# Two graph attention layers: the last two batches spread their head sums through TensorE

## Chip, core and metric

The kernel runs on one core of one Trainium2 chip. The metric is the device time of one execution in microseconds (us). It is given as the median of several runs; a profiled execution of the same program supplies the trace.

## What is computed

The input x holds 64 batches of 256 nodes with 512 features, and adj is one 256 x 256 adjacency matrix for all batches. Two layers follow each other, each with a layer norm in front and a residual around it. All is 32-bit floating point.

```python
h = relu(layernorm(x))                       # layer 0: graph attention
Wh = h @ W
logits = leaky_relu(Wh @ a_src [rows] + Wh @ a_dst [columns], 0.2)
x = x + softmax(where(adj, logits, -inf)) @ Wh

h = relu(layernorm(x))                       # layer 1: 8 heads of 64
q, k, v = h @ Wq.T + bq, h @ Wk.T + bk, h @ Wv.T + bv
attn = softmax(where(adj, q @ k.T / 8, -inf))   # per head
x = x + concat(attn @ v) @ Wo.T + bo
```

The change lies in the second half of layer 1: the division by the softmax sums, and the product with Wo.

## The kernel before

One batch is one group, so G is 64 and the groups are numbered 0 to 63. A group lives in a few stages, each written as a Python generator that issues some instructions and yields: loading, norms, edge weights and aggregation of layer 0 (`normalize0`, `weights0`, `aggregate0`, `transform0`), norm and transpose of layer 1 (`normalize1`, `transpose1`), projections (`project_qk`, `project_v`), `attention`, `scale` and `output`.

**The order is written by hand.** Lists such as `first_half` and `second_half` (L818 to L825) name stages with an offset: `(output, -2)` advances the output of the batch two behind the current one by one step. The loop at L845 walks through the lists for each iteration. Each engine then executes its own instructions strictly in the order in which they were issued, and waits where one needs data that is not there yet. An instruction that waits therefore holds up everything behind it on its engine.

**The seven products.** A product of 256 x 512 with a 512 x 512 weight is split into quarters and done with seven quarter products instead of eight. `combine` (L162) makes four sums of quarters of the left side (L167 to L170), on GpSimd except in batch 0. `products` (L173) issues the seven, each into one of eight PSUM banks. Two matmuls of L209 make one product of rows. VectorE adds each product to one or several quarters of the destination; for the output this is `add_to_rows` (L564).

**Attention.** For a pair of heads e, `scores` (L683) multiplies q and k into two PSUM banks (psc) and ScalarE takes the exponential into ex. `masks` (L701) multiplies ex by the mask twice (L703) and adds its two halves into sm (L705), on VectorE. `values(j)` (L708) multiplies two pairs of heads with v into pav, and ScalarE copies it to aT (L723). This is done for j = 0 and 1, so for four values of e, which hold eight heads. Before the second `values`, GpSimd adds the output bias to x (L734).

**Head sums.** After the second `values`, eight matmuls on 32 columns each (L742) sum sm over the nodes into psm: head pair e lands in rows 32e to 32e+31, sixteen equal rows for each of its two heads. VectorE takes the reciprocals rc (L750). SP then issues eight DMAs (L755), each of which reads one row of rc and writes it to the 64 partitions of a head in rb. In `scale`, VectorE multiplies aT by rb (L767), two operations of 128 x 512, and `combine` makes the quarter sums called as. `output` runs the seven products with Wo (po) and stores the two row blocks by DMA after the sixth and seventh (L780).

**The end.** In iterations 62 and 63 the same lists run, with the stages of missing batches left out. Iteration 64 runs `last` (L825):

```python
last = [A_OLD, A_OLD, A_OLD, O, O, O, O, O, O, O, AS]
```

A_OLD is the attention of the batch before, O the output of two before, AS the scaling of the batch before. So batch 63 finishes its attention, batch 62 then gets its seven outputs, and batch 63 is scaled; iteration 65 runs the ordinary lists once more, of which only the outputs of batch 63 are left.

## Time and profile before

| What | Value |
|---|---|
| median of 3 runs | 2987.39 us |
| lowest and highest | 2985.2, 2988.77 us |
| profiled run: time, span of the trace | 2984.37, 2982.6 us |
| mean granted TensorE clock | 0.993 |
| broadcasts rb<-rc (L755) | 512 of 64 KB, median 4.7 us from issue to landing |
| reciprocals (L750) | 64 of 1758 ns |
| masks (L703) | 512, mean 913 ns |
| scalings aT by rb (L767) | 128 of 128 x 512, mean 685 ns |
| additions of products (L564) | 889, mean 685 ns |

The span runs from the first to the last instruction. Engines are PE (matmuls of TensorE), PEld (its weight loads), DVE (VectorE), ACT (ScalarE), POOL (GpSimd) and SP (SyncE, here the queue that issues DMAs). Times within the trace count from the start of the span. In the trace every 32-bit matmul is recorded as two rows, so one product of L209 is four rows. The names are the program's; buffer numbers are left out, so that aT stands for both halves and all batches.

A line of a group shows what was written, what was read, the shape, the number, the busy time and the mean of one. Idle time before an instruction is put down to what came last. The chain of work that ended last is followed back from the final instruction, each step to what released it.

### The profile page before, as it was taken

To read this page: it belongs to the slowest core of one execution; us is meant where nothing else is said; L and a number is where in the kernel's file an instruction comes from. 1 tells how busy PE (TensorE), PEld (TensorE's weight loads), DVE (VectorE), ACT (ScalarE), POOL (GpSimd) and SP (SyncE) were. 2 spreads that over 40 slices of the span, in tenths; PEclk is the share of its full clock that TensorE was granted. 3 is DMA by queue.
4 is the path that set the end of the run, shared out by engine and by line. 5 is a ranking of instruction groups with operands and counts; after the bars stand their busy time and mean duration, and the time that the engine had idled before them with its cause. 6 is when DMAs were issued, how large, how long until landed. Compare 5 with 4: busy or idle time off the path is not lost.

```text
span 2982.6 us, 51508 instructions
## 1 busy us (share of the span) xinstructions
PE 2918.6 (98%) x19824; PEld 2496.8 (84%) x19824; DVE 2355.9 (79%) x3671; ACT 1252.3 (42%) x2972; POOL 1262.2 (42%) x1484
## 2 busy tenths in 40 slices
PE   5999999999999999999999999999999999999997
PEld 3878888888888888888888888888888888888885
DVE  3687888888888878878878878878878878878875
ACT  3444344344344443443443444444443443443431
POOL 2234544544544534534534534434435435435432
PEclk8999999999999999999999999999999999999999
DMA  4012122122122122122122122221221221221222
GB/s 141 12 33 43 29 36 43 29 36 43 26 40 37 28 43 36 30 44 35 31 43 33 32 43 32 34 43 31 35 43 30 36 43 29 36 43 30 29 29 37
DMA packets 83835, 112.46 MB, mean 38 GB/s; under 512 B 11906, under 2 KB 49794, under 8 KB 83586
## 3 DMA queue, kind: packets, MB, share of 16 engines
q1 hardware_dynamic: 82786, 107.00, 22.2%
q8 instruction: 160, 2.62, 0.3%
q0 software_dynamic: 800, 2.11, 0.2%
q14 instruction: 89, 0.73, 0.1%
HBM read 41.95 MB, written 33.55 MB: 25 GB/s over the span
## 4 chain that ended last, share of the span: by engine, by line
PE 96%; DVE 1%; DMA 1%; ACT 1%; POOL 0%; SPq 0%; issue 0%; DVEq 0%; POOLq 0%; ACTq 0%
PE pqk L218 27%; PE po L209 26%; PE pv L209 12%; PE psc L690 8%; PE pav L715 8%; PE pu L532 7%; PE psm L742 2%; PE pt L620 2%; PE ps L502 1%; PE prs L515 0%; PE pe L480 0%; SPq L755 0%; DMA rb<-rc 0%; DMA a_row<-in_L_gnn_a_dst_dram 0%; DVE x L564 0%
## 5 line engine op out<-in xcount | busy, mean ns | idle before, releaser
L564 DVE TENSOR_TENSOR x<-po,x 128x1024 f32<-128x1024 f32 x889 | 592.8, 685 | 113.5 <-PE po L209 93.4
L437 POOL TENSOR_SCALAR ve<-ssq 128x2 f32<-128x2 f32 x128 | 25.1, 196 | 1083.3 <-ACT h L426 803.5
L703 DVE TENSOR_TENSOR ex<-ex,maskT 128x512 f32<-128x512 f32 x512 | 447.0, 913 | 6.6 <-ACT ex L698 6.6
L698 ACT ACTIVATE ex<-psc 128x512 f32<-128x512 f32 x512 | 264.4, 603 | 124.0 <-PE psc L690 124.0
L723 ACT COPY aT<-pav 128x512 f32<-128x512 f32 x128 | 74.9, 585 | 524.2 <-PE pav L715 496.6
L218 PEld LDWEIGHTS pqk<-hs,wq_sb 128*128 128x128 f32 x2048 | 264.5, 192 | 9.8
L209 PE MATMUL po<-wo_sb,as 128*128 128x256 f32 x1024 | 269.1, 386 | 3.5 <-POOL as L168 3.5
L218 PE MATMUL pqk<-hs,wq_sb 128*128 128x128 f32 x2048 | 270.8, 276 | 0.0
L218 PE MATMUL pqk<-hs,wk_sb 128*128 128x128 f32 x2048 | 270.6, 275 | 0.0
L209 PE MATMUL pv<-wv_sb,hs 128*128 128x256 f32 x1024 | 263.8, 381 | 3.9 <-DVE x L564 3.9
L690 PE MATMUL psc<-qk 64*128 64x256 f32 x2048 | 255.8, 389 | 0.0
L466 DVE SCALAR_TENSOR_TENSOR junk<-h,wa 128x512 f32<-128x512 f32 x256 | 246.4, 963 | 11.6 <-ACT h L459 0.6
L715 PE MATMUL pav<-ex,v 128*64 128x256 f32 x2048 | 250.8, 386 | 4.3 <-DVE ex L703 4.3
L532 PE MATMUL pu<-em,h 128*128 128x256 f32 x1024 | 245.0, 383 | 8.4 <-POOL em L494 8.4
L649 ACT ACTIVATE p<-pqk,bias 128x128 f32<-128x128 f32 x256 | 73.0, 368 | 425.2 <-PE pqk L218 425.2
L218 PEld LDWEIGHTS pqk<-hs,wk_sb 128*128 128x128 f32 x2048 | 249.2, 192 | 0.0
L209 PE MATMUL po<-w_sb,us 128*128 128x256 f32 x1008 | 248.8, 380 | 0.0
L690 PEld LDWEIGHTS psc<-qk 64*128 64x128 f32 x2048 | 187.5, 187 | 67.6 <-ACT aT L723 25.9
L705 DVE TENSOR_TENSOR sm<-ex 128x512 f32<-128x512 f32 x256 | 228.3, 892 | 8.9
L750 DVE RECIPROCAL rc<-psm 128x256 f32<-128x256 f32 x64 | 112.5, 1758 | 155.1 <-PE psm L742 155.1
L532 PEld LDWEIGHTS pu<-em,h 128*128 128x128 f32 x1024 | 197.0, 193 | 36.1 <-POOL em L494 8.7
L167 POOL TENSOR_TENSOR hs<-hT 128x256 f32<-128x256 f32 x63 | 73.8, 1172 | 349.5 <-ACT hT L621 349.5
(193 smaller groups left out, 5953.5 us busy)
## 6 DMA issues: line engine op xcount, KB each, us to landing
x<-in_x_dram SPq DMA_DIRECT2D x64, 512.0 KB, 5.4
rb<-rc SPq DMA_DIRECT2D x512, 64.0 KB, 4.7
out_dram<-x SPq DMA_DIRECT2D x128, 256.0 KB, 2.0
wq_sb<-in_L_gnn_Wq_dram SPq DMA_DIRECT2D x4, 256.0 KB, 12.1
wk_sb<-in_L_gnn_Wk_dram SPq DMA_DIRECT2D x4, 256.0 KB, 10.1
w_sb<-in_L_gnn_W_dram SPq DMA_DIRECT2D x4, 256.0 KB, 6.6
wv_sb<-in_L_gnn_Wv_dram SPq DMA_DIRECT2D x4, 256.0 KB, 6.6
wo_sb<-in_L_gnn_Wo_dram SPq DMA_DIRECT2D x4, 256.0 KB, 6.0
```

Source lines behind the costliest of these rows:

```text
L209: nc.tensor.matmul(dst[:, 0:HD], left[:, c, :], wt[:, slot, c, :], start=c == 0, stop=c == 1)
L218: nc.tensor.matmul(dst[:, at : at + P], wt[:, slot, c, e * P : (e + 1) * P], left[:, c, :], start=c == 0, stop=c == 1,)
L466: nc.vector.scalar_tensor_tensor(junk, h[:, t, :], 1.0, wa[a], op0=ALU.mult, op1=ALU.mult, accum_out=dst[:, t : t + 1],)
L532: nc.tensor.matmul(pu[:, d, :], h[:, m, (dp + d) * P : (dp + d + 1) * P], em[:, m, :], start=(m == 0), stop=(m == NC - 1),)
L564: nc.vector.tensor_add(dst, src, dst)
L690: nc.tensor.matmul(psc[r][:, m, :], qk[rows, 2 + e % 2, m * P : (m + 1) * P], qk[rows, e % 2, :], start=True, stop=True,)
L698: nc.scalar.activation(ex[:, r, :, :], psc[r], AF.Exp, scale=SCALE)
L703: nc.vector.tensor_mul(ex[:, r, :, :], ex[:, r, :, :], maskT)
L705: nc.vector.tensor_add(sm, ex[:, :, 0, :], ex[:, :, 1, :])
L715: nc.tensor.matmul(pav[r * DH : (r + 1) * DH, i, :], v[j][:, m, at : at + DH], pair[i][:, r, m, :], start=(m == 0), stop=(m == NC - 1),)
L723: nc.scalar.copy(aT[j], pav)
L750: nc.vector.reciprocal(rc, psm)
```

## The change

It touches the last two batches, 62 and 63, and the order of the last iterations.

- A matrix pick (128 x 128) is made once, in the second iteration, by VectorE: in each block of 32 rows, its row 0 has ones in columns 0 to 63, and its row 16 has ones in columns 64 to 127.
- For batches 62 and 63 the eight DMAs are replaced by four matmuls, each with 32 rows of pick and 32 rows of rc, that write the reciprocals of a head pair to all 128 partitions of a PSUM bank (prb). Four of the eight banks hold them.
- `scale` then multiplies aT in four operations of 128 x 256 that read PSUM. The quarter sums of these two batches are made on VectorE.
- Head sums and reciprocals become a function, `head_sums`. For batch 63 it is called ahead of the second `values`, not after it.
- The step order: iteration 63 has a list of its own, in which the outputs of batch 62 (OL) stand between the value products, scores and masks of batch 63. The end is one iteration shorter. Its list, `end`, finishes batch 63.

```diff
-        def combine(a, name, g):
+        def combine(a, name, g, alone=False):
...
-            engine = nc.gpsimd if g else nc.vector
+            engine = nc.vector if alone or g == 0 else nc.gpsimd
...
+        pick = weights.tile([P, P], F32, tag="pick", name="pick")
+        def picks():
+            first = weights.tile([P, Q], F32, tag="first", name="first")
+            nc.vector.tensor_reduce(first, ident.rearrange("p (a q) -> p q a", q=Q), AX.X, ALU.add)
+            for r in range(2):
+                at = r * (Q // 2)
+                nc.vector.tensor_copy(
+                    pick[:, r * DH : (r + 1) * DH], first[:, at : at + 1].to_broadcast([P, DH])
+                )
...
             nc.vector.tensor_scalar(flag, pk, P - 0.5, None, op0=ALU.is_lt)
+            yield
+            picks()
+            yield
...
+                if j and g == G - 1:
+                    rc = head_sums(g, sums)
                 values(j, pair)
                 if j == 0:
                     yield
+            if g < G - 1:
+                rc = head_sums(g, sums)
+            if g < G - 2:
+                rb = work.tile([P, DC, N], F32, tag="rb", name=f"rb_{g}")
...
+            else:
+                yield
+                rb = [bank([P, N], f"prb_{g}_{e}") for e in range(DC)]
+                for e in range(DC):
+                    rows = slice(e * Q, (e + 1) * Q)
+                    nc.tensor.matmul(rb[e], pick[rows, :], rc[rows, :], start=True, stop=True)
+                outs[g] = aT, rb
+            yield
...
-            for j in range(2):
-                nc.vector.tensor_mul(aT[j], aT[j], rb[:, 2 * j : 2 * j + 2, :])
+            if g < G - 2:
+                for j in range(2):
+                    nc.vector.tensor_mul(aT[j], aT[j], rb[:, 2 * j : 2 * j + 2, :])
+            else:
+                for e in range(DC):
+                    part = aT[e // 2][:, e % 2, :]
+                    nc.vector.tensor_mul(part, part, rb[e])
...
-            outs[g] = a, combine(a, "as", g)
+            outs[g] = a, combine(a, "as", g, g >= G - 2)
...
-        last = [A_OLD, A_OLD, A_OLD, O, O, O, O, O, O, O, AS]
+        OL = (output, -1)
+        last = first_half + [
+            A_OLD, A, V, V, A, A_OLD, AS, V, V, V, OL, A, V, OL, V, OL, OL, A, A, OL, A, OL, OL, A,
+        ]
+        end = [A_OLD, A_OLD, AS, OL, OL, OL, OL, OL, OL, OL]
...
-        for i in range(G + 2):
+        for i in range(G + 1):
...
-            elif i == G:
-                todo = last
+            elif i >= G - 1:
+                todo = end if i == G else last
```

In the list `last`, A is the attention of batch 63: scores of the first four heads, two masks, values, scores of the other four, two masks. V is its value projection, and A_OLD and AS finish and scale batch 62.

## The prediction

> **What bounds the kernel now.** Three views, from coarse to fine. First the busy time of the page, then the clock row of its slices:

> ```profile
> PE 2918.6 (98%) x19824; PEld 2496.8 (84%) x19824; DVE 2355.9 (79%) x3671; ACT 1252.3 (42%) x2972; POOL 1262.2 (42%) x1484
> ...
> PEclk8999999999999999999999999999999999999999
> ```

> TensorE is busy from end to end. In the table by stretches, 100 to 2900 us has 2792 of 2800 us of matmuls at clock 1.00. Nothing that merely rearranges waits can pay there. The same table shows 15.6 of 20 us for 2940 to 2960 and 9.9 of 23 for 2960 to 2983, and the change works in exactly this tail. Second, the chain that ended last, cut to the tail (start, duration, what):

> ```profile
> 2934.88 0.47 SPq L755
> ...
> 2940.85 4.75 DMA rb<-rc
> ...
> 2945.82 0.69 DVE aT L767
> 2946.51 1.74 DVE ex L703 x2
> 2948.28 1.10 DVE sm L705
> 2949.38 2.27 DVE ex L703 x2
> ...
> 2954.47 1.77 DVE rc L750
> ...
> 2962.21 4.88 DMA rb<-rc
> ...
> 2967.32 0.70 DVE aT L767
> ...
> 2968.15 0.73 POOL as L167
> 2968.95 0.73 POOL as L168
> 2969.73 7.22 PE po L209 x24
> 2976.97 0.42 DVE x L564
> ```

> The reader is to see two round trips through the DMA queue, one for batch 62 and one for batch 63. VectorE makes the reciprocals, SP issues eight broadcasts (6.0 us from 2956.24 to 2962.21), the last needs 4.88 us to land, and only then does VectorE scale. GpSimd's sums follow. Third, what this does to TensorE's clock (stretch, its us, busy us of each engine, granted clock, DMA):

> ```profile
> 2944.00:2948.00 4.00, 1.64 (x12) 0.74 (x8) 2.18 (x3) 2.06 (x4) 1.27 (x2) 1.00 0.17 12
> ...
> 2964.00:2966.00 2.00, 1.80 (x4) 1.18 (x4) 0.05 (x1) 0.00 (x0) 0.00 (x0) 0.50 0.86 65
> ...
> 2970.00:2972.00 2.00, 2.00 (x5) 1.58 (x6) 0.16 (x1) 0.00 (x0) 1.04 (x2) 0.50 0.00 0
> ```

> The 3.5 us gap before 2964.20 left the clock at half, so most of the last seven products ran slowly. The 2.2 us gap at 2945 did not.

> [...] half after 3.5 us, full again at 2973.3. [...] the masks and sums of heads 4 to 7 take 6.90 us (2946.43 to 2953.33) beside GpSimd, where the same work for heads 0 to 3 took 3.9. [...] No row here shows row tiles of 32; psm, four column tiles of 32, does 16 rows in 1.0 us, which fits four at once.

> **The change part by part**, against the profiled span of 2982.6. Prices are distances between starts in the trace: a VectorE operation on 256 columns 0.34, on 512 0.60, on 1024 1.14, two masks and the wait of their sum 1.32 (2936.69 to 2938.01), a dependent 256-column step 0.46 (63.32 to 63.78); a product of L209 0.865; a VectorE reader starts 0.20 after such a product's slot, and TensorE 0.05 to 0.15 after VectorE's end.

> *Up to 2934.88 nothing moves.* The three operations that make pick run once in the second iteration. The trace has no reduction of that size; I bound the three between nothing and 1.2 us (a 128x512 sum averages 0.89, a 128x128 fill is 0.17, twice) and take nothing: TensorE leads there and VectorE idles 20%.

> *First stretch, VectorE's queue.* In front of the masks of batch 63 now stands s2v (L194), which waits for the second value product: 2934.88 + 2 x 0.865 + 0.20 = 2936.81. Before, the masks began at 2934.77; behind s2v wait both masks, sm and the four scalings. From 2936.81: s2v 0.34, masks 1.32, sm 0.60, four scalings out of PSUM (priced by L194, PSUM and SBUF in, 256 columns) 3 x 0.34 + 0.46, the four quarter sums 0.46 + 0.35 + 0.34 + 0.33, four value additions 0.34 + 0.46 + 0.34 + 0.34, the first output addition 1.14, masks 1.32, sm 0.60, the value addition L203 0.42: together 10.18, end 2946.99. TensorE meanwhile does pick's four matmuls (0.55 if four at once, 1.73 if one by one), three value products, then from the second scaling's end (2939.98) six products of 0.865 to 2945.17. With slow pick matmuls it would be 2946.1. Either way TensorE waits for L203, so their price is hidden here. The first value matmuls of heads 0 to 3 that need L203 start at 2947.14.

> *Second stretch.* Twelve of the sixteen pav rows 1.41, scores 1.93, the fifth output product 0.87 and 0.20 to its reader: 2951.55. On VectorE that addition stands ahead of the masks, which wait behind it although the exponentials of their first head pair are ready by 2950.8 (scores + 1.17, two of 0.52). Then 0.60 + 1.32 + 0.60 + 0.34 + 0.34 + 1.32 + 0.69 = 5.21, so the last sm ends at 2956.76 against 2953.33 before: **+3.43**. This is the price of moving seven outputs (6.05 us of TensorE, 4.24 of VectorE) out of the shadow of the second round trip, already net of the 3.0 us of GpSimd interference that goes with the quarter sums. GpSimd's bias addition for batch 63 moves up behind that of batch 62 (2.5 us from 2917.8), where TensorE hides it. Batch 62's two stores now meet an empty SP queue.

> *Third stretch, reciprocals to second output product.* From sm to reciprocals and their 1.77 us nothing changes: end 2959.67 instead of 2956.24. Before, 13.49 us passed from there to 2969.73. Now: pick's first matmul and its read 0.58, three more scalings 1.02, then 0.46 and 0.46 to the second quarter sum, its 0.42 and 0.11 to TensorE: 3.05; with pick's matmuls one by one 3.4. The value product moved behind the sums (1.88 from 2957.8, copy by ScalarE done at 2960.47) stays just inside. **-10.4** or **-10.1**.

> *Fourth stretch.* From the second output product to the last addition took 7.66 at half clock; six products at full clock are 5.19 + 0.20 + 0.42 = 5.81: **-1.85**. The 5.21 us from there to the end of the span stay.

> Sum: 3.43 - 10.44 - 1.85 = -8.9, or -8.5; I take **-8.7**, span 2973.9. The three timed runs lie between 2985.2 and 2988.8, the profiled one at 2984.4; from their median 2987.4 the forecast is **2978.7**. Within 0.2%, 6.0 us, a measurement of this kernel can hardly tell from no change.

> **The rivals.** *Half clock in the new gap.* From 2953.1 to 2956.9 TensorE has only three of eight psm matmuls, some 0.4 us. If that halves the clock, psm costs 0.56 more and pav runs until about 2962.0, when the clock returns; the scalings of its half wait, and the second output product starts at 2964.65 instead of 2962.7: gain 6.8, time 2980.6. If the outputs stay at half too, 2982.4. For it: 3.5 us sufficed before. Against: 2944 to 2952 had two such gaps and kept 1.00.

> *The interleaving costs more.* VectorE's queue is strict and I let it wait for TensorE only twice. If the whole moved output block stays uncovered, that is another 3 us or so (6.05 - 3.43 = 2.6, and small waits): 2981.7.

> *Slower.* The clock halves at the first wait (2945.2 to 2947.1) and the later gaps never let it recover. The chain then repeats its matmul time: 1.41 + 1.93 + 0.87 + 1.06 + 0.55 + 5.19 = 11.0, against a gain of 8.7: 2989.7. It decides once half clock covers 8.7 us of that chain. Against it: 2.2 us of gap kept full clock before.

> That the change might not act at all is excluded: the loop that issues the broadcasts now stands under g < G - 2.

> **How the numbers follow.** Forecast 0.55, half clock 0.22, costlier interleaving 0.18, slower 0.05. Faster by over 0.2% (under 2981.4): 0.55 + 0.14 + 0.05 = 0.74; within: 0.08 + 0.13 + 0.03 = 0.24; slower by more: 0.02. The range runs from 2976.0 (the forecast, the cheap bound, and the 1.8 us by which runs differ) to 2983.5 (both middle rivals, their halves at higher times).

> **What would show it.** Right: no transfer of rb after batch 61; s2v ahead of the masks at about 2936.8; the last sm some 3.4 us later than before; about 3 us from the reciprocals' end to the second output product; the last seven products at clock 1.00 and 0.87 apart. Wrong: VectorE waiting for output products more than twice before the last sm, pick's matmuls above 1.7 us, or a clock of 0.5 after 2953.

## The result and the profile after

The changed kernel took 2974.19 us (median of four runs, 2974.02 to 2977.06) against 2986.84 us beside it, a ratio of 0.996 [0.9942, 0.9977]. The forecast was 2978.7 us, the range 2976.0 to 2983.5: right in direction, but the time lies 1.8 us below the range. The same changed kernel was compared with the one before three more times (the last two beside the same runs of the kernel before), with medians of 2978.52, 2978.54 and 2979.21 us and ratios of 0.9975 [0.9966, 0.9983], 0.9971 [0.9961, 0.9982] and 0.9974 [0.9964, 0.9984]. So the forecast meets the time of the later comparisons, and the question is what made the first one 4 us shorter.

The page after, busy times:

```profile
PE 2917.0 (98%) x19840; PEld 2492.8 (84%) x19840; DVE 2355.8 (79%) x3686; ACT 1252.5 (42%) x2972; POOL 1254.1 (42%) x1476
```

TensorE has sixteen more rows (two times eight for pick), GpSimd lost the eight quarter sums, and nothing else is to be seen at this scale. The chain that ended last, cut to the tail (start, duration, what):

```profile
2938.16 0.42 DVE s2v L194
...
2948.40 1.52 PE pav L730 x12
...
2952.94 0.69 DVE x L579
...
2957.46 0.70 DVE sm L720
...
2958.20 1.05 PE psm L785 x10
2959.25 1.88 PE pav L730 x16
...
2961.20 0.72 PE prb L776 x8
...
2964.38 5.43 PE po L209 x24
...
2969.84 0.42 DVE x L579
```

Both DMA round trips are gone. Between the reciprocals and the second output product stands pick's matmul of 0.72 us where a transfer of 4.88 us stood. The stretch table (stretch, its us, busy us and rows of PE, PEld, DVE, ACT and POOL, granted clock, DMA share, GB/s) shows the last products at full clock; from 169 to 2974.5 us this trace has no half clock:

```profile
2964.00:2966.00 2.00, 1.62 (x8) 1.47 (x9) 2.00 (x4) 0.00 (x0) 0.00 (x0) 1.00 0.00 0
2966.00:2968.00 2.00, 2.00 (x11) 1.77 (x10) 1.90 (x4) 0.00 (x0) 0.00 (x0) 1.00 0.03 8
```

To compare executions I cut each at the first scores of batch 63 (psc, right behind the head sums of batch 62). What lies ahead is the **start and the body**, what lies behind is the **tail**. Before, the scores begin at 2932.95 and the tail is 49.65 us. After, they begin at 2934.13, although the only work added far ahead of them is pick, and the tail is 40.87. (Spans are read to 0.1 us, so a tail is good to about 0.05.) The tail became 8.8 us shorter, for 8.7 forecast. What the forecast did not see is that the place of the scores is not a constant.

### The profile page after: what moved, and what is told of

Its sections match the earlier page's. It is cut to its first block, busy times and chain, and to the rows that moved or that the text cites. A ratio compares the mean times of both kernels' runs of the same rounds, so it can differ in the third digit from the quotient of the medians.

```text
span 2975.0 us, 51505 instructions
## 1 busy us (share of the span) xinstructions
PE 2917.0 (98%) x19840; PEld 2492.8 (84%) x19840; DVE 2355.8 (79%) x3686; ACT 1252.5 (42%) x2972; POOL 1254.1 (42%) x1476
## 4 chain that ended last, share of the span: by engine, by line
PE 96%; DVE 2%; ACT 1%; DMA 1%; POOL 0%; issue 0%; DVEq 0%; POOLq 0%; ACTq 0%
PE pqk L218 27%; PE po L209 26%; PE pv L209 12%; PE psc L705 8%; PE pav L730 8%; PE pu L547 7%; PE psm L785 2%; PE pt L635 2%; PE ps L517 1%; PE prs L530 0%; PE pe L495 0%; DVE x L579 0%; DMA a_row<-in_L_gnn_a_dst_dram 0%; DVE ex L718 0%; PE pgram L352 0%
## 5 line engine op out<-in xcount | busy, mean ns | idle before, releaser
L209 PE MATMUL po<-wo_sb,as 128*128 128x256 f32 x1024 | 268.3, 385 | 0.9 <-DVE as L168 0.9
L209 PE MATMUL pv<-wv_sb,hs 128*128 128x256 f32 x1024 | 263.4, 380 | 3.1 <-DVE x L579 3.1
L705 PE MATMUL psc<-qk 64*128 64x256 f32 x2048 | 256.0, 389 | 0.0
L209 PE MATMUL po<-w_sb,us 128*128 128x256 f32 x1008 | 248.6, 379 | 0.0
L705 PEld LDWEIGHTS psc<-qk 64*128 64x128 f32 x2048 | 187.5, 187 | 68.2 <-ACT aT L738 25.9
L167 POOL TENSOR_TENSOR hs<-hT 128x256 f32<-128x256 f32 x63 | 73.7, 1170 | 349.3 <-ACT hT L636 349.3
```

Of the source, the lines that this page charges most:

```text
L209: nc.tensor.matmul(dst[:, 0:HD], left[:, c, :], wt[:, slot, c, :], start=c == 0, stop=c == 1)
L705: nc.tensor.matmul(psc[r][:, m, :], qk[rows, 2 + e % 2, m * P : (m + 1) * P], qk[rows, e % 2, :], start=True, stop=True,)
```

## The experiments

Two theories of the missing 4 us were open after the result. A: the start of the program takes a different time in each execution. B: the tail of the kernel before is often longer than in its profile. A rival, C: something that the change adds shortens the start. The parts of the tail were tested beside them.

**Both kernels unchanged, and pick alone.** The third kernel is the one before with pick made and not used:

```diff
+        pick = weights.tile([P, P], F32, tag="pick", name="pick")
+        def picks():
...
+            yield
+            picks()
+            yield
```

> The kernel before, unchanged. I split a span into the lead, up to the first scores of batch 63 (right behind the head sums of batch 62), and the tail after it. In the traces at hand the lead is 2933.0 (before) and 2934.1 (after), the tail 49.7 and 40.9: the tail gains 8.8 as forecast, while the medians of time differ by 12.7. Theory A (the lead varies from execution to execution by some 2 us either way, for instance with the phase of TensorE's clock in the first 200 us, and four executions of each kernel happened to differ): tail 49.7 again within 0.5, lead anywhere from 2931 to 2936, ratio to the kernel before 1.000. Theory B (the tail of before is often longer than the profiled one): tail clearly above 50.2, lead 2933.0 within 0.5. Theory C (something that the change adds shortens the lead): says nothing of this run.

> The changed kernel, unchanged. Theory A: tail 40.9 within 0.5, lead 2931 to 2936, and over more executions the gain in time falls towards 8.8, say 8 to 11. Theory B: tail 40.9, and the gain stays near 12.7. Theory C: lead below the lead of before in most executions, gain stays near 12.7.

> The kernel before plus the three VectorE operations that make pick (not used) and their two steps. Theories A and B: same time as before within 1.5 us (my prediction priced them at nothing, at most 1.2 us slower). Theory C with pick as its cause: about 4 us faster than before.

Measured: 2985.8 us, ratio 1.0001 [0.9992, 1.0009]; 2978.52 us, 0.9975 [0.9966, 0.9983]; 2987.67 us, 1.0005 [0.9997, 1.0013]. The scores came at 2934.44, 2936.42 and 2935.46 us, the tails were 49.56, 40.88 and 52.14 us. A holds: the scores move by 3.5 us over the five profiles so far, the tail of the change by less than 0.05. C is not borne out: the changed kernel, with all that it adds, had the latest scores of all. With pick alone the median is 1.5 us above the kernel before, which its interval does not tell from nothing. The traces settle it: from the second scores of batch 1 to its head sums, the stretch in which pick is made, it is 23.91 us with pick alone and 23.76 and 23.99 us in the two profiles without pick. B holds in part: one execution of the old tail is 2.5 us longer, with a clock of 0.50 behind a gap at 2948 to 2952.

**The old order of steps**, with the reciprocals still spread by TensorE and the quarter sums on VectorE:

```diff
-        last = first_half + [
-            A_OLD, A, V, V, A, A_OLD, AS, V, V, V, OL, A, V, OL, V, OL, OL, A, A, OL, A, OL, OL, A,
-        ]
-        end = [A_OLD, A_OLD, AS, OL, OL, OL, OL, OL, OL, OL]
+        at = second_half.index(AS)
+        near_last = first_half + second_half[:at] + [A_OLD] + second_half[at:]
+        last = [A_OLD, A_OLD, A_OLD, O, O, O, O, O, O, O, A_OLD, AS]
```

The lines show the two lists; the loop has its 66 iterations again, and the head sums of batch 63 stand behind its second values again, too.

> The changed kernel with the order of steps of before: all of masks, values and sums of batch 63 first, then the seven outputs of batch 62, then pick's matmuls and scaling of batch 63; pick, the scaling from PSUM and the quarter sums on VectorE stay. My theory says that moving the outputs forward costs 3.4 us, since they used to stand in the shadow of a round trip that is now gone: tail about 37 (the last sm some 8 us earlier than in the changed kernel, seven products of 0.865 behind it, then 3 us to the second output product). Its rival, that the outputs between values and scores are part of the gain: tail above 40.9, time slower than the changed kernel by 2 us or more.

Measured: 2974.82 us, 0.9965 [0.9952, 0.9979], tail 38.1 us. It beats the change by 3.7 us in the same comparison. Seen from the scores, the last sm ends at 16.4 us here and at 24.0 in the change, 7.6 later. From the reciprocals' end to the second output product of batch 63 it is 7.55 here and 3.33 in the change, 4.2 less. The other two pieces give 0.6 back. The new order, with the early head sums, is a loss of 2.8 us.

**The quarter sums back on GpSimd**, in the old order:

```diff
-            outs[g] = a, combine(a, "as", g, g >= G - 2)
+            outs[g] = a, combine(a, "as", g)
```

> The old order of steps with the reciprocals spread by TensorE, as in the run with the old order, but the quarter sums of batches 62 and 63 on GpSimd again. Theory (the sums of batch 62 on GpSimd hold up the masks of heads 4 to 7, 6.9 instead of 3.9 us in the kernel before, and those of batch 63 are 0.73 us each instead of 0.34 to 0.46): tail 38.1 + 2 to 3.5, that is 40 to 41.6, time 2977 to 2978. Rival (VectorE is the bound of the tail, and gains what GpSimd takes over, 2 x 1.5 us): tail 37 or less.

Measured: 2978.93 us, 0.9977 [0.9969, 0.9985], tail 41.45 us, inside the theory's 40 to 41.6; the time is 0.9 us above what it expected. The parts are now separate, each as a difference of profiled tails: TensorE's spreading of the reciprocals, with the four scalings that read it and the full clock of the last products, 49.6 to 41.45 (-8.2), the sums on VectorE 41.45 to 38.1 (-3.3), the new order 38.1 to 40.9 (+2.8).

**The two waits of VectorE removed** from the changed kernel, by order alone:

```diff
-            A_OLD, A, V, V, A, A_OLD, AS, V, V, V, OL, A, V, OL, V, OL, OL, A, A, OL, A, OL, OL, A,
+            A_OLD, A, A, V, V, A_OLD, AS, V, V, V, OL, A, V, OL, V, OL, OL, A, A, A, OL, OL, OL, A,
```

> The change with two entries of its hand-written order exchanged twice: the masks of heads 0 to 3 of batch 63 stand ahead of its first value products (so the addition s2v no longer holds them), and the masks of its third head pair stand ahead of the fifth output addition of batch 62. The same instructions, only their order on VectorE differs. In the changed kernel VectorE idled 2.1 us ahead of s2v and 2.5 us ahead of that addition. Theory (these two waits are the price of the interleaving): the tail, 40.9 us from the scores of batch 63 to the end, becomes about 38 (37.4 to 38.9), so some 2978 - 3 = 2975 to 2976 us beside runs of the changed kernel of that chip. Rival (VectorE's work, not its waits, sets the end, so that a wait removed only moves into the next one): tail 40 or more.

Measured: 2975.95 us, 0.9961 [0.9948, 0.9975], tail 40.27 us. The time met the expectation, but the profiled tail lies where the rival had put it, and only the profile says why. The last sm ends 21.5 us after the scores instead of 24.0, so 2.5 us of waiting are gone. The timeline of this kernel (start, duration, engine, line, operation, count, idle before and its releaser) shows what took them back:

```profile
2957.00 1.05 PE L785 MATMUL psm<-sm,half 128*32 128x256 f32 x10 [1.88 <-DVE sm L720]
2957.98 3.48 PE L730 MATMUL pav<-ex,v 128*64 128x256 f32 x16
```

The sixteen rows of the last values took 3.48 us instead of 1.95: the granted clock was 0.50 for 3.41 us from 2958.23 on, behind a gap of 1.88 us. No profile caught this order at full clock there, so that its tail would then be near 38 us is not shown.

**b_v loaded earlier.** It has nothing to do with the tail; it changes the start of the changed kernel, where the transfer of b_v waits for a buffer that it shares with the rows brow:

```diff
-                row = work.tile([1, D], F32, tag="b12", name=f"brow_{j}", bufs=2)
+                row = work.tile([1, D], F32, tag="brow", name=f"brow_{j}", bufs=2)
```

> The changed kernel, but the two rows brow have buffers of their own, so that the transfer of b_v in the second iteration no longer waits until VectorE has read them. Nothing of the tail differs. In the changed kernel VectorE waited 4.9 us for b_v at 145 us and TensorE ran at 0.91 of its clock in 140 to 180. Theory (the start, up to about 194 us, is what varies from execution to execution, through such waits and the half clock after them): b_v lands before it is needed, no wait of VectorE of over 1 us at L405, clock 0.97 or more in 140 to 180, first scores of batch 63 some 3 to 5 us earlier than 2934 to 2936, tail 40.9 as before, time 2973 to 2976. Rival (the start is bound by something else): the scores within 1.5 us of where they were and the time within 1.5 us of the changed kernel's.

Measured: 2973.4 us, 0.9956 [0.9942, 0.997]. The scores came at 2930.03 us, 4.1 to 6.4 earlier than in the two profiles of the changed kernel at hand, as expected. The rest missed its expectation, and taught more than the part that met it: the clock is 1.00 in 140 to 160 but 0.92 in 160 to 180, and the tail is 42.87 us, 2.0 longer with the very same instructions. The stretch table cut at the clock's own steps, first this kernel, then the changed one:

```profile
2951.94:2955.35 3.41, 1.44 (x15) 0.58 (x16) 2.23 (x5) 0.00 (x0) 0.00 (x0) 1.00 0.41 154
2955.35:2958.76 3.41, 3.41 (x20) 1.74 (x20) 1.59 (x1) 0.14 (x1) 0.00 (x0) 0.50 0.00 0
```

```profile
2954.06:2957.48 3.42, 1.75 (x9) 0.45 (x7) 3.35 (x8) 0.00 (x0) 0.00 (x0) 1.00 0.21 77
2957.48:2960.89 3.41, 2.69 (x26) 1.44 (x26) 2.27 (x2) 0.00 (x0) 0.00 (x0) 1.00 0.21 76
```

The same gap of 1.97 us ahead of the head sums lies in both. Cut one way, a step has 1.44 us of matmuls (42%) and the next runs at half; cut the other way it has 1.75 us (51%) and the next stays at full clock.

**The gap filled** in that kernel, with products whose result is overwritten:

```diff
             psm = bank([P, N], f"psm_{g}")
+            if g == G - 1:
+                for _ in range(5):
+                    nc.tensor.matmul(psm, ident, bo_b[:, 0:N], start=True, stop=True)
```

> The kernel of the run with b_v early, and in front of the head sums of batch 63 five idle products (identity times a constant, 128x256 each, into the bank that the head sums then overwrite), so that TensorE doesn't stand still while VectorE finishes the last masks. In that run TensorE's clock was at half for 3.4 us behind this gap, and the tail was 42.9 us instead of the 40.9 of both profiles of the changed kernel. From ten profiles: in each, the clock changes only at times that lie whole multiples of 3.413 us apart, and goes to half where TensorE was busy for less than about half of such a cell. Theory (the same gap costs nothing or 2 us, by how it lies in these cells): with the gap filled no cell of the tail up to the last product is at half, tail 40.8 to 41.3, and no timed run stands about 2 us above the lowest through its tail: median 2970.9 to 2972. Rival (the half clock comes from something other than the gap): half clock in the same place, tail 42.9.

Measured: tail 41.06 us, full clock up to the last product, as expected. The median is 2973.02 us (2970.61 to 2973.83; 0.9951 [0.9938, 0.9965]), 1 us above what was expected of it: the tail of its one profile is settled, yet the runs still spread by 3 us. That the gap was filled mattered here: with the five products taken off the records, the step of the clock from 2947.29 us would have been busy for 39%, an estimate; with them it was busy throughout. With its early b_v this profile has its scores at 2927.74, 2.3 us ahead of the other with the same start.

**b_k and b_v early**, in the changed kernel:

```diff
-                w_q = whole((wq_sb, wk_sb)[n], (wqT, wkT)[n], "qk"[n])
+                w_q = w_k if n else whole(wq_sb, wqT, "q")
...
                 yield
+                if n == 0:
+                    w_k = whole(wk_sb, wkT, "k")
...
+            wv_q = whole(wv_sb, wvT, "v")
             nc.vector.tensor_scalar(ok[:, 0 : 2 * DC], rows, 0.66, None, op0=ALU.is_le)
```

and bufs=3 for the tag b12.

> The changed kernel with three buffers instead of two for b_q, b_o, b_k, b_v and the rows brow, and the transfers of b_k and b_v issued earlier in the program, so that neither TensorE (2.5 us at 120, for b_k) nor VectorE (4.9 us at 145, for b_v) waits for them. The tail is as in the change. Theory (these waits and the half clock behind them are what makes the start long and different from execution to execution): no wait for b_k or b_v of over 1 us, first scores of batch 63 at 2926 to 2928.5 instead of 2934.1 to 2936.4, tail 40.9 or 42.9 by the place of the gap in the clock's cells, time 2967 to 2972. Rival (a wait removed there only moves on to the next one, as to that for xn at 160): scores at 2929.5 or later.

Measured: 2970.15 us (2969.05 to 2970.99), 0.9943 [0.9929, 0.9956], scores at 2926.12, tail 41.08. The start is 8 us or more shorter than the changed kernel's, and the five runs spread by 1.9 us.

**The changed kernel twice more**, to see its start and tail again:

> The changed kernel once more, on another chip than before. Theory (only the start and the place of the gap in the clock's cells differ from execution to execution): first scores of batch 63 between 2931 and 2936.5, tail 40.9 (or 42.9 with half clock behind the gap ahead of the head sums), and time = scores + tail + 1.9 to 2.1 us; timed runs between 2974 and 2980. Rival (the tail itself varies in other ways): a tail below 40.5 or between 41.3 and 42.4.

> The same kernel a second time, for another profile: the same two expectations. If the theory holds, the difference of the two profiled spans is that of the times of the first scores to within 0.3 us, but for a step of 2 us where one has half clock in the tail.

Measured: 2978.54 and 2979.21 us, scores at 2935.04 and 2934.59, tails 40.86 and 40.81. The difference of the spans, 0.5 us, is that of the scores. One of the nine executions of the second took 10659.24 us; no profile caught it, and it stays unexplained. The ratio leaves it out.

**A better tail.** Three kernels tried to run the outputs of batch 62 on TensorE while VectorE scales batch 63, in the old order:

```diff
-        last = [A_OLD, A_OLD, A_OLD, O, O, O, O, O, O, O, A_OLD, AS]
+        last = [A_OLD, A_OLD, O, A_OLD, O, A_OLD, AS, O, O, O, O, O]
```

> The old order of steps with the reciprocals spread by TensorE and the quarter sums on VectorE, but of the seven outputs of batch 62 one stands ahead of the last values of batch 63, one ahead of the spreading matmuls and five behind its scaling, so that outputs 3 to 7 run on TensorE while VectorE scales. Theory (with the old order TensorE waits for VectorE's scaling of batch 63, and VectorE idles 1.5 us ahead of the reciprocals): from the reciprocals' end 12 products of 0.865 us and their reading, tail 36.4 (35.8 to 37.2), time 1.0 to 2.2 us below the old order's, some 2973. Rival (the additions become the bound on VectorE and TensorE waits for banks): tail 37.5 or more, no gain over the old order.

Measured: 2976.18 us, 0.9967 [0.9955, 0.998], tail 39.54 us: worse than the old order's 38.1, so the theory missed. In the timeline two of the four scalings wait for ScalarE's copy of the last values, and the additions pile up behind them:

```profile
2959.54 0.75 DVE L801 TENSOR_TENSOR aT<-aT,prb 128x256 f32<-128x256 f32 x2 [3.61 <-ACT aT L738]
...
2961.87 6.98 DVE L579 TENSOR_TENSOR x<-po,x 128x256 f32<-128x256 f32 x12
```

The second half of aT has one buffer, which the outputs of batch 62 still read. With a second one (bufs=2 for tag aT1):

> The run with split outputs, with two buffers instead of one for the second half of aT. In that run ScalarE's copy of the last values of batch 63 came at the end of the outputs of batch 62, which still read that buffer, and the scalings of its heads 4 to 7 waited 3.6 us for it; then twelve additions in a row on VectorE set the end. Theory (this buffer is what spoiled the split): no wait of the scalings for ScalarE of over 0.5 us, the last product of TensorE bounds again, tail 36.7 (36.2 to 37.4) against 38.1 for the old order and 39.5 for the split. Rival (VectorE's work is the bound in any order): tail 38 or more.

Measured: 2975.46 us, 0.9963 [0.995, 0.9977], tail 39.03 us, a miss again, and the wait has moved one step on:

```profile
2957.15 0.42 DVE L167 TENSOR_TENSOR as<-aT,aT 128x256 f32<-128x256 f32 x1 [3.15 <-PE po L209]
```

The quarter sums as have one buffer, too, read by the same outputs. Together with the early start this gave

> Both together: the start as in the run with early b_k and b_v, the tail as in the split with two buffers. If start and tail are independent, first scores of batch 63 at 2926 to 2928.5, tail 36.7 (36.2 to 37.4), time 2964 to 2967.5, below both kernels by over 0.2%.

Measured: 2967.85 us, 0.9934 [0.992, 0.9948], scores at 2926.19 and tail 39.41, so start and tail add up to within 0.4 us of the two apart, but the tail is not the 36.7 hoped for. With the sums of batch 63 in the buffer of another tile (tag hs) that is free by then:

> As the run with early start and split outputs (tail 39.4, not the 36.7 expected: the quarter sums of batch 63 waited 3.2 us for the outputs of batch 62 to have read their one buffer, and behind them twelve additions ran on VectorE alone), but the sums of batch 63 go into the buffer of another tile of the same size that is free by then. Theory (buffers, not VectorE's work, set the end): no wait of the sums for outputs of batch 62, the last product of TensorE followed within 1 us by the last addition, tail 37.0 (36.5 to 37.6), time 1.8 to 2.9 us below that run's 2967.85 as measured beside the kernel before, that is 2965 to 2966. Rival (VectorE's additions set the end in any order): tail 38.5 or more.

Measured: 2965.24 us (2963.2 to 2965.5), 0.9925 [0.9912, 0.9938], tail 36.36 us, slightly better than expected. Its last two rows show TensorE's products setting the end, with VectorE right behind:

```profile
2957.50 0.42 DVE L584 TENSOR_TENSOR x<-po,x 128x256 f32<-128x256 f32 x1 [0.17 <-PE po L212]
2958.36 0.42 DVE L584 TENSOR_TENSOR x<-po,x 128x256 f32<-128x256 f32 x1 [0.44 <-PE po L212]
```

This version beats both kernels: 21.8 us below the one before, and 13.3 and 14.0 us below the two changed kernels measured beside it.

## Why the prediction was right in its steps and wrong in its range

The steps of the tail, with the profile after shifted so that its first scores fall on those of before (-1.19 us):

| Step of the prediction | forecast | measured |
|---|---|---|
| s2v (ahead of the masks) starts | 2936.81 | 2936.97 |
| L203 ends | 2946.99 | 2947.15 |
| values that need it start | 2947.14 | 2947.21 |
| last sm ends | 2956.76 (+3.43) | 2956.96 (+3.63) |
| reciprocals' end to second output product | 3.05 (-10.44) | 3.33 (-10.16) |
| from there to the last addition's end | 5.81 (-1.85) | 5.88 (-1.78) |
| from there to the end of the span | 5.21 | 4.74 (-0.47) |
| sum | -8.9, taken -8.7 | -8.8 |

The sum is closer than its parts: three terms came out 0.07 to 0.28 us dearer than forecast, together 0.55, and 0.47 us less from the last addition to the end, which the prediction held fixed, made up for most of it. That much is luck.

**Right.** Pick's four matmuls on 32 rows each ran together: four rows start within 0.02 us, and all eight take 0.71 us, where the prediction put 1.73 for one by one. The 0.55 for four at once was an estimate of mine, which no row of the trace before showed for 32 rows; measured, the four are 2.4 times as fast as one by one, and the price was 0.16 us too low. Pick itself is free, as far as the traces show. The 3.0 us put down to GpSimd are to be seen in VectorE's operations: before, beside GpSimd's additions, the two pairs of masks of heads 4 to 7 took 1.82 and 2.34 us and their sums 1.10 and 1.65; after, with GpSimd idle from 2921.41 us on, each pair took 1.28 and each sum 0.69. VectorE waited for TensorE twice, ahead of s2v and of the fifth addition, as the queue argument said:

```profile
2938.16 0.42 DVE L194 TENSOR_TENSOR s2v<-v,pv 128x256 f32<-128x256 f32 x1 [2.13 <-PE pv L209]
...
2952.94 0.69 DVE L579 TENSOR_TENSOR x<-po,x 128x512 f32<-128x512 f32 x1 [2.47 <-PE po L209]
```

The masks stood behind the first wait although their data was there: ScalarE's four exponentials of heads 0 to 3 ended at 2937.36, and the masks began at 2938.50, right behind s2v. That these two waits hold up the last sm is shown by the run that removed them (last sm 2.5 us earlier). That the moved outputs are a price and not a gain is shown by the old order.

**The rival of half clock** was given 0.22 and came true in some executions rather than in the kernel: not in four profiles of the changed kernel, but in the one with b_v early, which has the same tail, at 2.0 us, for the 1.9 that its price said. That price had the clock come back at 2962.0, which was an estimate: in the trace before, half clock had lasted 10.24 us (2963.08 to 2973.32), and with b_v early it lasted 3.41. The argument against it, that two earlier gaps had kept full clock, was no argument: those cells were 50% and 52% busy, and in another execution of the same tail, the run with pick alone, one was at 44% and the clock did halve. An estimate from the records of the changed tail: of all the places where the clock's grid of 3.413 us steps could cut it, some 60% leave a step under 46% busy. This suggests that 0.22 was low, but six profiles with this tail (four of the changed kernel and the two with only its start altered), with one such case, are too few to say how often it happens.

**The step that failed** is the last: the lower end of the range, "the forecast, the cheap bound, and the 1.8 us by which runs differ". The term of 1.8 us was half the spread of three runs of the kernel before, and behind it stood the sentence that up to 2934.88 nothing moves. It moves, by 4.35 us. (The two terms that have a size, -8.9 in place of -8.7 and the 1.8 us, give 2976.7 where the range has 2976.0; the measured 2974.19 lies below both.) The profiles of kernels with an unaltered start:

| Kernel | steps at half clock in 40-75, 115-130, 145-200 us | first scores | tail |
|---|---|---|---|
| split, two buffers | 5, 0, 1 | 2932.07 | 39.03 |
| before | 7, 1, 1 | 2932.95 | 49.65 |
| changed, fourth | 7, 1, 1 | 2934.59 | 40.81 |
| split | 7, 1, 1 | 2934.66 | 39.54 |
| after | 5, 1, 2 | 2934.13 | 40.87 |
| before, again | 5, 1, 2 | 2934.44 | 49.56 |
| changed, third | 5, 1, 2 | 2935.04 | 40.86 |
| two waits removed | 5, 1, 2 | 2935.43 | 40.27 |
| pick alone | 5, 1, 2 | 2935.46 | 52.14 |
| old order | 5, 1, 2 | 2935.98 | 38.1 |
| sums on GpSimd | 5, 1, 2 | 2936.25 | 41.45 |
| changed, again | 5, 1, 2 | 2936.42 | 40.88 |

The scores range over 4.35 us. From the second head sums (psm of batch 1, 189.7 to 194.5 us) to these scores it is 2741.7 to 2742.4 us in all of them, so nearly all of it arises in the first 195 us. The stretch table of two of them, first split with two buffers, then changed, third, shows one such difference, clock 1.00 and 0.97 against 0.89 and 0.94:

```profile
115.00:130.00 15.00, 11.41 (x102) 11.20 (x101) 6.71 (x13) 1.58 (x9) 9.82 (x11) 1.00 0.06 19
145.00:200.00 55.00, 49.69 (x319) 40.68 (x318) 45.35 (x89) 19.63 (x46) 15.99 (x21) 0.97 0.22 38
```

```profile
115.00:130.00 15.00, 11.58 (x90) 11.37 (x89) 6.81 (x13) 1.43 (x8) 9.82 (x11) 0.89 0.06 19
145.00:200.00 55.00, 49.34 (x311) 40.15 (x310) 41.95 (x87) 19.39 (x47) 14.61 (x19) 0.94 0.20 34
```

Fewer halved steps behind 115 us go with earlier scores: one with 2932.1, two with 2933.0 to 2934.7, three with 2934.1 to 2936.4. The three timed runs that set the median of the result had spans of 2972.1 to 2972.4 us; with the tail of 40.9 that every profile of the changed kernel shows, their scores would have come near 2931.3. Their mean clock is listed as 0.996, that of the profiled run as 0.995; one halved step costs 1.7 of 2975 us, or 0.0006 of the mean. This fits, but it is weak: two later runs of the changed kernel are listed at 0.996 too, and took 2977.48 and 2978.1 us. The kernel before has such short executions as well: of its 76 timed runs in the later comparisons three took 2981.4 to 2982.0 us, each at least 2.3 us below the next in its comparison; with the tail of 49.6 of its two profiles, their scores would have come near 2930. So an early start does not seem to need the change. All this is worked out: no profile caught such an execution, and why three of four fell there in the first comparison, and none of the 27 later runs of the changed kernel (the one of 10659 us left out), stays open.

One trace cannot give the start's spread, but the trace before had a warning: the clock of 0.91 in 120 to 140 us and 0.93 in 140 to 160, and the waits for transfers of b_k and b_v near by:

```profile
122.42 0.68 PE L340 MATMUL pgram<-b_k 128*128 128x128 f32 x4 [2.30 <-DMA b_k<-in_L_gnn_Wk_dram]
...
150.72 0.43 DVE L393 SCALAR_TENSOR_TENSOR sqv<-b_v 128x256 f32<-128x256 f32 x1 [4.40 <-DMA b_v<-in_L_gnn_Wv_dram]
```

The run with both loaded early, whose scores come at 2926.12, shows what these waits and the half clock around them are worth: 8.0 us against the profile after.

## What to carry to other kernels

Before a gain of some microseconds is forecast, take several profiles of the kernel before, cut each at a point ahead of the change, and see whether that point stands still from one execution to the next; a median of a few runs inherits whatever moves there. A gap on TensorE had two prices here, nothing or 2 us (tails of 40.87 and 42.87), depending on where the clock's grid cut it, so give both, with the busy share of the worst and the best cut. And work moved out of the shadow of a wait is only worth it if that wait is not itself going away: here the outputs of batch 62 cost less where they had been, ahead of pick's matmuls (tail 38.1 for 40.9), and least with five of the seven behind the scaling, once two buffers no longer held batch 63 back (36.4).

## What the hardware showed

**The way back took more.** Three steps at half clock in the tail that were busy for 60%, 60% and 67% were followed by another at half; behind 100 us, those busy for 83% and more were all followed by full clock. The prediction's reading of the trace before, half after 3.5 us and full again at 2973.3, leaves this out: the last seven products began at 2964.20, and three steps at half, busy for 60%, 5% and 100%, passed before full clock came back.
